# Two attention layers on one core: a new order of the side work in the first seven steps, and a last batch whose halves lie in separate PSUM banks

## The chip, the core and the metric

The kernel runs on one core of one Trainium2 chip. The core has five engines that each work through a queue of their own in order: TensorE (PE in the profile, its weight loads PEld), VectorE (DVE), ScalarE (ACT), GpSimd (POOL) and SyncE (SP, which here only starts DMAs). They wait for one another through semaphores. Matmul results land in PSUM, eight banks of 128 partitions x 512 fp32 values, from where DVE and ACT copy them to SBUF. The metric is the device time of one execution in microseconds (us).

## What is computed

Two cross-attention layers follow each other for 8 batches of 256 tokens with 320 channels, in fp32, with 20 heads of 16 channels. The context has 256 rows of 512 channels. Layer 0 attends to 77 text rows and 179 image rows with two separate softmaxes and adds the two results. Layer 1 attends to 252 text rows; its 4 image rows get scores to which a semantic term is added, and a mask per token.

```python
# layer 0
q, k, v       = heads(x @ Wq.T), heads(text @ Wk.T), heads(text @ Wv.T)
k_ip, v_ip    = heads(ip @ Wk_ip.T), heads(ip @ Wv_ip.T)
x1 = (attend(q, k, v) + attend(q, k_ip, v_ip)) @ Wo.T + bo + x
# layer 1
probs_t  = softmax(q1 @ k_t.T * scale)
text_out = probs_t @ v_t
qsem     = l2norm(probs_t @ text_ehs)
fused    = q1 @ k_ip.T * scale + 0.5 * (qsem @ l2norm(ip_ehs).T)
probs_ip = softmax(fused) * spatial_mask[:, None]
out = (text_out + probs_ip @ v_ip) @ W_out + b_out + x1
```

The norm of qsem is not computed from qsem itself: the kernel multiplies the probabilities with the Gram matrix of the text rows (l1_gram) and sums the product with the probabilities.

## The kernel before

The 20 heads of a batch are cut into five quads of four heads. The main loop runs over n = 0 to 45. Step n < 40 does quad n % 5 of batch n // 5 in layer 0, and layer 1 follows six steps behind (SHIFT), so that steps 6 to 39 do a quad of each layer (both_layers) and steps 40 to 45 only layer 1 (layer_1). After the loop, l1_end finishes the last batch.

A layer-0 step goes as follows. The scores of four heads are computed on TensorE into four PSUM banks sc0 to sc3 (line 359), from queries that POOL has masked (qz, line 349). DVE takes maxima (500), ACT exponentials (512), TensorE transposes the probabilities in the same banks (397), DVE copies three heads and ACT the fourth to SBUF (404, "et"), and l0_values multiplies them with v (530, "oT"), which ACT copies to SBUF (540). The next step transposes that result back (550, "o"). Layer 1 has the same frame; its products y (752, 755) take value and Gram columns together from the tile gv, and DVE reads y (759, 763).

Everything that is not a step of a quad is a filler: projections (l0_q, l0_k, l0_v, l1_q, l1_k, l1_v), Gram matrices (l1_gram), the projections of the image rows for all batches at once (ip_squares, ip_norm, ip_T, ip_k, ip_v), and the ends of batches (l0_attn_T, l0_out, l1_probs, l1_probs_T, l1_text, l1_attn, l1_out). The function fillers(n, place) holds a table of places by step, written by hand; steps 0 to 7 have tables of their own. In both_layers place 0 comes after the scores, maxima and half of the exponentials of the step, place 1 after the first two transposed heads and l0_attn, place 2 after the last two. Directly after place 2 the kernel issues the masked queries on POOL, those of layer 1 for this step and those of layer 0 for the next one:

```python
        fillers(n, 2)
        part(l1_values, v1, 2)
        qz[1] = queries(1, n)
        qz[0] = queries(0, n + 1)
```

l1_gram(b, c) works on one half of the 252 text rows: four matmuls (621), ACT multiplies of the result into gv (630; three for c = 0, one for c = 1), and a POOL copy that repeats these columns for the other nine pairs of heads (634; 3402 columns for c = 0, 1134 for c = 1). ip_norm takes a square root on ACT, which loads another activation table (250). The order of PE, DVE, ACT and POOL is as written in the code; the framework sets the waits. Small PSUM results share two banks (mm_tile).

l1_end adds text and image results in PSUM. Its steps text, image, keep and project handle both halves (two times 128 tokens): text transposes attention rows into a bank, image adds the image rows' part, keep copies the sums to SBUF, half 0 on DVE and half 1 on ACT, and project multiplies with the output weights. Heads 0 to 15 (chunks 0 and 1) are done first, heads 16 to 19 (chunk 2) last. Both halves' sums lie in one bank, and so do both halves of pT, the transposed image probabilities.

Of the kernel before, what the change touches and what calls it, by code (L numbers as in the profile page):

```python
# [8 lines left out]
F32 = mybir.dt.float32  # L9
AF = mybir.ActivationFunctionType  # L10
ALU = mybir.AluOpType
# [39 lines left out]
def kernel(  # L51
# [40 lines left out]
    def mm_tile(name):  # L92
        return ps_mm.tile([P, 512], F32, tag="mm", name=name)
# [515 lines left out]
    def l1_gram(b, c):  # L609
        r = bat[b]  # L610
        encT_b = r["encT"]
        if c == 0:
            r["gv"] = [
                bp.tile([TC1, NPAIR, w + 2 * WV], F32, tag=f"gv{i}", name=f"gv{i}_{b}")
                for i, w in enumerate((3 * TC1, TC1))
            ]
        gv = r["gv"][c]
        ps = mm_tile(f"g{c}_{b}")
        n = TXT1 - c * TC1
        for k in range(NE):  # L620
            nc.tensor.matmul(  # L621
                ps[:TC1, :n],
                encT_b[:, k, c * TC1 : (c + 1) * TC1],
                encT_b[:, k, c * TC1 : TXT1],
                start=(k == 0),
                stop=(k == NE - 1),
            )
        blocks = ((TC1, 2.0), (0, 1.0), (TC1, 2.0)) if c == 0 else ((0, 1.0),)
        for i, (t0, f) in enumerate(blocks):
            nc.scalar.mul(  # L630
                gv[:, 0, WV + i * TC1 : WV + (i + 1) * TC1], ps[:TC1, t0 : t0 + TC1], f
            )
        n = len(blocks) * TC1
        nc.gpsimd.tensor_copy(
            gv[:, 1:, WV : WV + n],
            bc(gv[:, 0, WV : WV + n].unsqueeze(1), [TC1, NPAIR - 1, n]),
        )
# [98 lines left out]
    def l1_transposed(u, j, copy=None):  # L736
        transposed_probs(u, j, TC1, u["t0"][j // 2], copy)
# [35 lines left out]
    def by_n(t):  # L773
        n = t.shape[2]
        return bc(t.unsqueeze(3), [P, NH, n, NIP])
# [40 lines left out]
    def l1_probs(b, hs=ALL, eng=nc.gpsimd):  # L816
        r = bat[b]
        fus, g = r["fus"][:, :, hs, :], by_head(r, "gip", b)
        nc.vector.tensor_reduce(g[:, :, hs], fus, AX.X, ALU.add)
        nc.vector.reciprocal(g[:, :, hs], g[:, :, hs])  # L820
        for half in range(NH):
            eng.tensor_scalar_mul(g[:, half, hs], g[:, half, hs], msk[:, half : half + 1])
        eng.tensor_tensor(fus, fus, by_n(g[:, :, hs]), ALU.mult)
# [14 lines left out]
                ALU.mult,  # L838
            )

    def l1_probs_T(b, hs=ALL, ps=None, shared=False):
        r = bat[b]

        rows = hs.stop * NIP
        if ps is None:
            ps = mm_tile(f"pT_{b}")
        for half in range(NH):
            nc.tensor.transpose(
                ps[:rows, half * P : (half + 1) * P],
                r["fus"][:, half, : hs.stop, :].rearrange("p h k -> p (h k)"),  # L850
                ident,
            )
        if "pT" not in r:
            r["pT"] = small.tile([H * NIP, NH * P], F32, tag="pT", name=f"pT_sb_{b}", bufs=1)
        if shared:
            for copy, cols in ((nc.vector.tensor_copy, slice(0, P)), (nc.scalar.copy, slice(P, 2 * P))):
                copy(r["pT"][:rows, cols], ps[:rows, cols])
        else:
            nc.vector.tensor_copy(r["pT"][:rows], ps[:rows, : NH * P])

    def l1_attn(b):
        r = bat[b]
# [24 lines left out]
    def l1_end(b, u):  # L887

        r = bat[b]
        first, last = slice(0, 16), slice(16, H)

        def tile(j, name):
            return ps_sc.tile([P, NH * S], F32, tag=f"sc{j}", name=f"end_{name}")

        def values(j, half):
            l1_values(u, j, (half,))

        def chunk(t, m):
            return t[:, CH[m] : CH[m] + P]

        def text(ps, piece, i, start):
            m, half = piece
            nc.tensor.matmul(
                ps[:, i * P : (i + 1) * P], chunk(r["attn1"][half], m), ident,
                start=start, stop=False,
            )

        def image(ps, ms, hs):
            rows = hs.stop * NIP
            vip = r["vip"].rearrange("p h d -> p (h d)")[:rows]
            for i, m in enumerate(ms):
                nc.tensor.matmul(
                    ps[:, i * S : (i + 1) * S], chunk(vip, m), r["pT"][:rows],
                    start=False, stop=m == ms[-1],
                )

        def keep(ps, ms):  # L920
            n = len(ms)
            v = ps[:, : n * S].rearrange("p (m n s) -> p m n s", m=n, n=NH)
            for half, copy in enumerate((nc.vector.tensor_copy, nc.scalar.copy)):
                copy(aT[half][:, ms[0] : ms[0] + n, :], v[:, :, half, :])

        def project(half, m):
            nc.tensor.matmul(
                o[half][:, :C], aT[half][:, m, :], wo1[:, m, :], start=(m == 0), stop=(m == 2)
            )

        aT = [
            work.tile([P, NC, P], F32, tag="aT", name=f"end_aT_{half}", bufs=2)
            for half in range(NH)
        ]
        o = [tile(2 + half, f"o_{half}") for half in range(NH)]
        sums, sums2 = tile(0, "aT"), mm_tile("end_aT2")
        texts = [(m, half) for m in (0, 1) for half in range(NH)]
        l1_norm(b, first)
        values(0, 0)
        l1_fused(b, first)  # L940
        values(0, 1)
        l1_text(b, first)
        values(1, 0)
        l1_fused_exp(b, first)
        table(AF.Sqrt)
        values(1, 1)
        values(2, 0)
        l1_probs(b, first)
        for i in range(len(texts)):
            text(sums, texts[i], i, i == 0)  # L950
            if i < 3:
                values(*((2, 1), (3, 0), (3, 1))[i])
        l1_norm(b, last)
        l1_text(b, last)
        l1_probs_T(b, first, tile(1, "pT"))
        l1_fused(b, last, nc.vector)
        l1_fused_exp(b, last, nc.vector)
        image(sums, (0, 1), first)
        keep(sums, (0, 1))
        l1_probs(b, last, nc.vector)  # L960
        for half in range(NH):
            text(sums2, (2, half), half, half == 0)
        project(0, 0)
        project(0, 1)
        l1_probs_T(b, last, tile(1, "pT2"), True)
        project(1, 0)
        project(1, 1)
        sums = sums2
        image(sums, (2,), last)
        keep(sums, (2,))  # L970
        for half, eng in enumerate((nc.sync, nc.scalar)):
            project(half, 2)
            osb = work.tile([P, C], F32, tag="attn1", name=f"osb_{b}_{half}", bufs=3)
            nc.vector.tensor_tensor(osb, o[half][:, :C], r["x1"][:, half, :], ALU.add)
            eng.dma_start(out=out[b, half * P : (half + 1) * P, :], in_=osb)
# [24 lines left out]
    def fillers(n, place):  # L1000
# [30 lines left out]
        if n <= NQ + 2:  # L1031
# [3 lines left out]
                    1: [(l0_v, 0, 2)],  # L1035
                },
                {
                    0: [(l0_k, 0, 1)],
                    1: [(l0_k, 0, 2)],
                    2: [(l0_q, 0, (2,))],  # L1040
                },
                {
                    0: [(l1_gram, 0, 0), (l0_v, 1, 0)],
                    1: [(l0_k, 1, 0), (ip_squares, 0)],
                    2: [(ip_norm, 0)],
                },
                {
                    0: [(l0_v, 1, 1), (l0_q, 1, (0, 1))],
                    1: [(ip_T, 0), (l0_v, 1, 2)],
                    2: [(ip_v, 0)],  # L1050
                },
                {
                    0: [(l1_ip, 0), (l1_v, 0, 0), (l1_v, 0, 1)],
                    1: [(ip_k, 0), (l1_gram, 0, 1)],
                    2: [(ip_k, 1)],
                },
                {
                    0: [(l0_k, 1, 1), (ip_k, 2), (l0_q, 1, (2,))],
                    1: [(l1_k, 0, 0)],
                    2: [(l0_attn_T, 0, 0), (l0_attn_T, 0, 1), (l0_out, 0, 0), (l0_out, 0, 1)],  # L1060
                    5: [(l1_xT, 0)],
                    6: [(l1_q, 0, (0, 1))],
                },
                {
                    0: [(l1_k, 0, 1)],
                    1: [(l1_q, 0, (2,))],
                    2: [(l0_k, 1, 2)],
                    4: [(l1_ip, 1), (l1_gram, 1, 0)],
                    5: [(l1_gram, 1, 1)],
                },  # L1070
# [24 lines left out]
            plan[3, 4] = [(l1_k, now, 0)]  # L1095
            plan[4, 0] = [(l1_v, now, 0)]
        if b == B:
            plan[0, 4] = [(l1_k, last, 1)]
            plan[1, 4] = []
        for f, at, *args in plan.get((s, place), ()):  # L1100
            if 0 <= at < B:
# [69 lines left out]
    def layer_1(n, u, v1):  # L1171
# [17 lines left out]
        for pair in range(2):  # L1189
            for head in (2 * pair, 2 * pair + 1):  # L1190
                l1_transposed(u1, head, nc.scalar.copy)
            if n == N0 + SHIFT - 1 and pair:
                l1_den(B - 1)
            part(l1_values, v1, 2 + pair)
            fillers(n, 5 + pair)
# [81 lines left out]
```

## Time and profile before

| | |
|---|---|
| median of three runs | 883.96 us (883.8 to 883.97) |
| the profiled execution, own time | 883.8 us |
| its span in the profile | 882.1 us |
| TensorE busy | 865.1 us |
| VectorE busy | 614.0 us |
| ScalarE busy | 546.0 us |
| GpSimd busy | 208.8 us |
| DMA queues, share of 16 engines, all four | 9.3% |

The profile is of one execution. Its own time is 1.7 us longer than its span, which begins with the first record and ends with the last. A row of a timeline gives the start in us from the begin of the span, the duration, the engine, the line, the operation, the tile written and the tiles read, the shape, the count of merged instructions, and in brackets the idle time ahead of it with what ended it. An fp32 matmul appears as two passes (x2), a transpose as one. Ends of matmuls are modelled, so distances from start to start are safer than durations. In the table of windows, the columns are the window, its length, the busy time of PE, PEld, DVE, ACT and POOL with their counts, the granted TensorE clock, the busy share of the DMA engines and GB/s.

### The profile page before, as it was taken

The numbers are of one execution on the slowest core, as the hardware profiler recorded it, in microseconds if no ns is written. First come the engines' busy times: TensorE is split into PE (matmuls) and PEld (weight loads), VectorE is DVE, ScalarE is ACT, GpSimd is POOL, SyncE is SP. The second block draws the span as 40 slices with busy tenths as digits, with TensorE's granted clock in tenths as the row PEclk, the third lists the DMA queues.
The fourth block names the chain that finished last, engine by engine and source line by source line (L and its number), as shares of the span: only waits on it lengthen the run. The fifth ranks groups of instructions, "written<-read, shape, count | busy, mean of one in ns | idle before, by whom it ended". The sixth has DMA issues, their size and how long they took to land.

```text
span 882.1 us, 18743 instructions
## 1 busy us (share of the span) xinstructions
PE 865.1 (98%) x6178; PEld 696.4 (79%) x6178; DVE 614.0 (70%) x2071; ACT 546.0 (62%) x2386; POOL 208.8 (24%) x376
## 2 busy tenths in 40 slices
PE   9999899999999999999999999999999999999997
PEld 6767678788787887888878888888888787777776
DVE  2544477767777777776778678776777778775765
ACT  4765666656755586555765468654675558654844
POOL 2212311223221222122321322212232122312111
PEclk9999999999999999999999999999999999999999
DMA  9600100001000100011001010000100100000000
GB/s 278 173 6 6 52 2 1 2 16 43 15 2 20 34 25 2 10 27 42 16 1 21 16 43 1 3 20 16 43 1 1 22 16 1 1 21 1 1 20 16
DMA packets 24624, 22.96 MB, mean 26 GB/s; under 512 B 5936, under 2 KB 24496, under 8 KB 24528
## 3 DMA queue, kind: packets, MB, share of 16 engines
q1 hardware_dynamic: 23088, 20.27, 8.7%
q10 hardware_dynamic: 1440, 1.49, 0.5%
q8 instruction: 50, 0.82, 0.4%
q14 instruction: 46, 0.38, 0.1%
HBM read 18.31 MB, written 2.62 MB: 24 GB/s over the span
## 4 chain that ended last, share of the span: by engine, by line
PE 85%; ACT 3%; DVE 1%; issue 0%; POOL 0%; ACTq 0%; DVEq 0%
PE y L752 17%; PE sc L397 15%; PE sc L359 9%; PE y L755 9%; PE v L322 9%; PE k L310 7%; PE q L292 6%; PE p_o L335 5%; PE oT L530 4%; PE g L621 2%; ACT e L728 1%; ACT e L512 1%; PE p_aT_ps L328 1%; PE o L550 1%; PE ipo L866 1%; PE x1T_ps L328 1%
## 5 line engine op out<-in xcount | busy, mean ns | idle before, releaser
L512 ACT ACTIVATE e<-sc,nmx 128x77 f32<-128x77 f32 (+1 forms) x640 | 227.2, 411 | 58.1 <-DVE nmx L500 56.4
L728 ACT ACTIVATE e<-sc,nmx 128x252 f32<-128x252 f32 x320 | 147.4, 484 | 119.5 <-DVE aip L708 106.2
L752 PE MATMUL y<-gv,et 126*128 126x272 f32 x640 | 202.1, 397 | 1.2
L759 DVE CUSTOM_DVE_ANT_0 e<-y,e 128x252 f32<-128x252 f32 x320 | 134.0, 419 | 93.2 <-PE y L755 84.9
L397 PE MATMUL sc<-ident,e 128*126 128x128 f32 (+1 forms) x1280 | 183.2, 274 | 6.2 <-ACT e L512 3.7
L404 DVE COPY et<-sc 128x512 f32<-128x512 f32 (+1 forms) x228 | 153.9, 689 | 24.7 <-PE sc L397 15.5
L500 DVE TENSOR_REDUCE nmx<-sc 128x2 f32<-128x154 f32 x320 | 109.7, 415 | 85.4 <-PE sc L359 85.4
L397 PEld LDWEIGHTS sc<-ident,e 128*126 128x126 f32 (+1 forms) x1280 | 148.7, 140 | 17.6 <-ACT e L512 8.2
L512 ACT ACTIVATION_READ_ACCUMULATOR e<-sc,nmx 128x1 f32 x640 | 159.5, 250 | 0.0
L755 PEld LDWEIGHTS y<-gv,et 126*128 126x128 f32 x640 | 120.7, 189 | 25.9
L755 PE MATMUL y<-gv,et 126*128 126x146 f32 x640 | 131.4, 287 | 0.0
L713 DVE TENSOR_REDUCE nmx<-sc 128x2 f32<-128x504 f32 x160 | 106.7, 674 | 24.2 <-PE sc L359 24.2
L565 POOL TENSOR_TENSOR attn<-o_sb 128x64 f32<-128x64 f32 x80 | 24.4, 327 | 405.4 <-DVE o_sb L555 365.5
L752 PEld LDWEIGHTS y<-gv,et 126*128 126x128 f32 x640 | 104.8, 190 | 18.1 <-issue 3.0
L404 ACT COPY et<-sc 126x512 f32<-126x512 f32 (+1 forms) x92 | 52.9, 593 | 74.2 <-PE sc L397 74.1
L359 PE MATMUL sc<-k,sc_qz 32*128 32x256 f32 x1152 | 82.5, 400 | 1.0 <-POOL sc_qz L349 1.0
L349 POOL TENSOR_SCALAR sc_qz<-q,quad_m 128x256 f32<-128x256 f32 x80 | 73.2, 925 | 7.3 <-ACT q L299 6.7
L359 PEld LDWEIGHTS sc<-k,sc_qz 32*128 32x128 f32 x1152 | 52.0, 184 | 24.4 <-issue 14.8
L728 ACT ACTIVATION_READ_ACCUMULATOR e<-sc,nmx 128x1 f32 x320 | 69.8, 218 | 0.0
L322 PE MATMUL v<-wv,encT 128*126 128x324 f32 (+1 forms) x192 | 58.1, 447 | 0.0
L763 DVE COPY num<-y 128x20 f32<-128x20 f32 x320 | 55.8, 174 | 0.0
L335 PE MATMUL p_o<-wo,p_aT 128*128 128x320 f32 x180 | 53.0, 437 | 0.3 <-DVE p_aT L329 0.3
(151 smaller groups left out, 1047.1 us busy)
## 6 DMA issues: line engine op xcount, KB each, us to landing
encT<-in_encT_dram SPq DMA_DIRECT2D x7, 512.0 KB
x<-in_x_dram SPq DMA_DIRECT2D x8, 320.0 KB
out_dram<-osb SPq DMA_DIRECT2D x15, 160.0 KB
xT<-in_xT_dram SPq DMA_DIRECT2D x7, 256.0 KB
texts<-in_encT_dram SPq DMA_DIRECT2D x6, 154.0 KB
xT<-in_xT_dram SPq DMA_DIRECT2D x7, 128.0 KB
vip_rows<-vipA SPq DMA_DIRECT2D x32, 25.0 KB
wv<-in_WvT_dram SPq DMA_DIRECT2D x1, 640.0 KB
```

What stands on the lines that cost most here:

```text
L322: nc.tensor.matmul(ps, lhsT(k), w[:, k, :], start=(k == 0), stop=(k == NE - 1))
L335: nc.tensor.matmul(ps[:, :C], aT[:, m, :], w[:, m, :], start=(m == 0), stop=(m == NC - 1))
L359: nc.tensor.matmul(sc[j][:, half, :], qz[rows, half * P : (half + 1) * P], kT(j)[rows, :], start=True, stop=True,)
L397: nc.tensor.transpose(v[:, c, half, :], u["e"][x][:, i, half, t0 + c * tn : t0 + (c + 1) * tn], ident,)
L404: copy(u["et"][x][:tn, i].rearrange("p c n s -> p (c n s)"), ps)
L500: nc.vector.tensor_reduce(u["nmx"][x][:, j, :, a], u["sc"][2 * x + j][:, :, t0:t1], AX.X, ALU.max, negate=True,)
L512: nc.scalar.activation(u["e"][x][:, j, half, t0:t1], u["sc"][2 * x + j][:, half, t0:t1], AF.Exp, bias=u["nmx"][x][:, j, half, a : a + 1], ...
L713: nc.vector.tensor_reduce(u["nmx"][x][:, j, :], u["sc"][2 * x + j][:, :, t0 : t0 + TXT1], AX.X, ALU.max, negate=True,)
L728: nc.scalar.activation(u["e"][x][:, j, half, t0 : t0 + TXT1], u["sc"][2 * x + j][:, half, t0 : t0 + TXT1], AF.Exp, bias=u["nmx"][x][:, j, ...
L752: nc.tensor.matmul(y, et[:, 1 - odd, half, :], gv[0][:, g, full], start=True, stop=False)
L755: nc.tensor.matmul(y[:, into], et[:, odd, half, :], gv[1][:, g, part], start=False, stop=True)
L759: nc.vector.tensor_tensor_reduce(e, y[:, g0 : g0 + TXT1], e, op0=ALU.mult, op1=ALU.add, scale=1.0, scalar=0.0, accum_out=r["n2"][:, half, ...
```

## The change

It has two parts. The first deals out the fillers of steps 1 to 6 anew. The q projection of columns of chunk 2 goes from place 2 to place 0 of step 1, l1_gram(0, 1) from place 1 of step 4 to place 2 of step 1, l1_gram(0, 0) from place 0 to place 2 of step 2, and further projections come one place or one step earlier or later. l1_gram allocates gv at whichever of its calls comes first.

```diff
                 {
-                    0: [(l0_k, 0, 1)],
+                    0: [(l0_k, 0, 1), (l0_q, 0, (2,))],
                     1: [(l0_k, 0, 2)],
-                    2: [(l0_q, 0, (2,))],
+                    2: [(l1_gram, 0, 1)],
                 },
                 {
-                    0: [(l1_gram, 0, 0), (l0_v, 1, 0)],
+                    0: [(l0_v, 1, 0), (l0_v, 1, 1)],
                     1: [(l0_k, 1, 0), (ip_squares, 0)],
-                    2: [(ip_norm, 0)],
+                    2: [(ip_norm, 0), (l1_gram, 0, 0)],
                 },
                 {
-                    0: [(l0_v, 1, 1), (l0_q, 1, (0, 1))],
-                    1: [(ip_T, 0), (l0_v, 1, 2)],
+                    0: [(l0_q, 1, (0, 1)), (ip_T, 0)],
+                    1: [(l0_v, 1, 2)],
                     2: [(ip_v, 0)],
                 },
                 {
                     0: [(l1_ip, 0), (l1_v, 0, 0), (l1_v, 0, 1)],
-                    1: [(ip_k, 0), (l1_gram, 0, 1)],
-                    2: [(ip_k, 1)],
+                    1: [(ip_k, 0), (ip_k, 1)],
+                    2: [(ip_k, 2)],
                 },
                 {
-                    0: [(l0_k, 1, 1), (ip_k, 2), (l0_q, 1, (2,))],
+                    0: [(l0_k, 1, 1), (l0_q, 1, (2,))],
                     1: [(l1_k, 0, 0)],
...
                 {
-                    0: [(l1_k, 0, 1)],
-                    1: [(l1_q, 0, (2,))],
-                    2: [(l0_k, 1, 2)],
+                    0: [(l1_k, 0, 1), (l1_q, 0, (2,))],
+                    1: [(l0_k, 1, 2)],
```

The second part concerns the steps after layer 0 has ended, and l1_end. In step 40, l1_k of the last batch's second chunk goes from place 4 to place 0, ahead of the o transposes (l0_attn). In step 43, l1_probs_T and l1_text of batch 6 go from place 5, between the two pairs of heads, to a new place 7 behind the transposes of the second pair.

```diff
         if b == B:
-            plan[0, 4] = [(l1_k, last, 1)]
+            plan[0, 0] = [(l1_k, last, 1)]
+            plan[0, 4] = []
+            plan[3, 7], plan[3, 5] = plan[3, 5], []
             plan[1, 4] = []
...
                 l1_transposed(u1, head, nc.scalar.copy)
+            if pair:
+                fillers(n, 7)
```

In l1_end, the sums of the two halves get a bank each (sc0 and sc1 for chunks 0 and 1, the two mm banks for chunk 2), and so do the two halves of the last pT (the two banks of y). Each half's copy follows its own transposes. image issues one matmul of 128 columns per half and chunk instead of one of 256 per chunk. Two texts come ahead of the value product (2, 1) instead of one. image and keep of chunk 2 come ahead of project(1, 1) instead of behind it. Where l1_probs runs on DVE (the last four heads), mask and 1/sum are applied by one fused instruction per half, in place of two multiplies of the sums and one of the probabilities.

```diff
+        if eng is nc.vector:
+            for half in range(NH):
+                f = fus[:, half]
+                eng.scalar_tensor_tensor(
+                    f, f, msk[:, half : half + 1], by_n(g[:, :, hs])[:, half], ALU.mult, ALU.mult
+                )
+            return
...
-        for i in range(len(texts)):
-            text(sums, texts[i], i, i == 0)
-            if i < 3:
-                values(*((2, 1), (3, 0), (3, 1))[i])
+        text(sums, 0, 0)
+        text(sums, 0, 1, 1)
+        values(2, 1)
+        text(sums, 1, 0)
+        values(3, 0)
+        text(sums, 1, 1, 1)
+        values(3, 1)
...
-        l1_probs_T(b, last, tile(1, "pT2"), True)
+        l1_probs_T(
+            b, last,
+            [ps_y.tile([P, W2], F32, tag="y", name=f"end_pT2_{half}") for half in range(NH)],
+            copies,
+        )
         project(1, 0)
+        image(sums2, (2,), last)
+        keep(sums2, (2,))
         project(1, 1)
-        sums = sums2
-        image(sums, (2,), last)
-        keep(sums, (2,))
```

More of the change, by code (lines that the diff above doesn't have):

```diff
@@ L611, in l1_gram @@
         encT_b = r["encT"]
-        if c == 0:
+        if "gv" not in r:
             r["gv"] = [
@@ L839, in l1_text, with l1_probs_T @@
             )
-    def l1_probs_T(b, hs=ALL, ps=None, shared=False):
+    def l1_probs_T(b, hs=ALL, ps=None, copies=None):
         r = bat[b]
         rows = hs.stop * NIP
+        whole = mm_tile(f"pT_{b}") if ps is None else None
         if ps is None:
-            ps = mm_tile(f"pT_{b}")
+            ps = [whole[:, half * P : (half + 1) * P] for half in range(NH)]
+        if "pT" not in r:
+            r["pT"] = small.tile([H * NIP, NH * P], F32, tag="pT", name=f"pT_sb_{b}", bufs=1)
         for half in range(NH):
             nc.tensor.transpose(
-                ps[:rows, half * P : (half + 1) * P],
+                ps[half][:rows, :P],
                 r["fus"][:, half, : hs.stop, :].rearrange("p h k -> p (h k)"),
@@ L852, in l1_probs_T @@
             )
[L853 to L859, printed above, removed]
+            if copies:
+                copies[half](r["pT"][:rows, half * P : (half + 1) * P], ps[half][:rows, :P])
+        if not copies:
+            nc.vector.tensor_copy(r["pT"][:rows], whole[:rows, : NH * P])
     def l1_attn(b):
@@ L902, in chunk, with text @@
             return t[:, CH[m] : CH[m] + P]
-        def text(ps, piece, i, start):
-            m, half = piece
+        copies = (nc.vector.tensor_copy, nc.scalar.copy)
+        def text(ps, half, m, i=0):
             nc.tensor.matmul(
-                ps[:, i * P : (i + 1) * P], chunk(r["attn1"][half], m), ident,
-                start=start, stop=False,
+                ps[half][:, i * P : (i + 1) * P], chunk(r["attn1"][half], m), ident,
+                start=i == 0, stop=False,
             )
@@ L913, in image @@
             vip = r["vip"].rearrange("p h d -> p (h d)")[:rows]
[L914 to L918, printed above, removed]
+            for half in range(NH):
+                for i, m in enumerate(ms):
+                    nc.tensor.matmul(
+                        ps[half][:, i * P : (i + 1) * P], chunk(vip, m),
+                        r["pT"][:rows, half * P : (half + 1) * P],
+                        start=False, stop=m == ms[-1],
+                    )
         def keep(ps, ms):
             n = len(ms)
-            v = ps[:, : n * S].rearrange("p (m n s) -> p m n s", m=n, n=NH)
-            for half, copy in enumerate((nc.vector.tensor_copy, nc.scalar.copy)):
-                copy(aT[half][:, ms[0] : ms[0] + n, :], v[:, :, half, :])
+            for half, copy in enumerate(copies):
+                copy(
+                    aT[half][:, ms[0] : ms[0] + n, :],
+                    ps[half][:, : n * P].rearrange("p (m s) -> p m s", m=n),
+                )
         def project(half, m):
@@ L935, in l1_end @@
         o = [tile(2 + half, f"o_{half}") for half in range(NH)]
-        sums, sums2 = tile(0, "aT"), mm_tile("end_aT2")
-        texts = [(m, half) for m in (0, 1) for half in range(NH)]
+        sums = [tile(half, f"aT_{half}") for half in range(NH)]
         l1_norm(b, first)
@@ L948, in l1_end @@
         l1_probs(b, first)
-        for i in range(len(texts)):
-            text(sums, texts[i], i, i == 0)
-            if i < 3:
-                values(*((2, 1), (3, 0), (3, 1))[i])
+        text(sums, 0, 0)
[5 more added lines that the diff above has]
+        values(3, 1)
         l1_norm(b, last)
         l1_text(b, last)
-        l1_probs_T(b, first, tile(1, "pT"))
+        l1_probs_T(b, first)
         l1_fused(b, last, nc.vector)
@@ L960, in l1_end @@
         l1_probs(b, last, nc.vector)
+        sums2 = [mm_tile(f"end_aT2_{half}") for half in range(NH)]
         for half in range(NH):
-            text(sums2, (2, half), half, half == 0)
+            text(sums2, half, 2)
         project(0, 0)
         project(0, 1)
-        l1_probs_T(b, last, tile(1, "pT2"), True)
+        l1_probs_T(
+            b, last,
+            [ps_y.tile([P, W2], F32, tag="y", name=f"end_pT2_{half}") for half in range(NH)],
+            copies,
+        )
         project(1, 0)
+        image(sums2, (2,), last)
+        keep(sums2, (2,))
         project(1, 1)
-        sums = sums2
-        image(sums, (2,), last)
-        keep(sums, (2,))
         for half, eng in enumerate((nc.sync, nc.scalar)):
```

## The prediction

> **What bounds the kernel now.** I read the busy table first, then the chain that ended last, then busy time by step. TensorE works 98% of the span and is 85% of the chain, so time is lost or won only where TensorE stands still.
>
> ```profile
> PE 865.1 (98%) x6178; PEld 696.4 (79%) x6178; DVE 614.0 (70%) x2071; ACT 546.0 (62%) x2386; POOL 208.8 (24%) x376
> ...
> PE 85%; ACT 3%; DVE 1%; issue 0%; POOL 0%; ACTq 0%; DVEq 0%
> ```
>
> The view by windows, cut where each step's scores start (steps 1 to 6 of the main loop), has as columns: window, length, busy PE, PEld, DVE, ACT, POOL, granted clock, DMA share, GB/s.
>
> ```profile
> 22.50:33.66 11.16, 10.27 (x90) 8.53 (x89) 5.31 (x13) 8.79 (x40) 1.50 (x3) 1.00 0.87 227
> 33.66:44.90 11.24, 11.19 (x83) 8.52 (x83) 7.03 (x15) 8.86 (x40) 5.57 (x7) 1.00 0.44 113
> 44.90:59.70 14.80, 14.29 (x95) 9.84 (x95) 7.56 (x19) 9.62 (x40) 3.29 (x6) 1.00 0.00 1
> 59.70:71.38 11.68, 11.40 (x92) 8.79 (x91) 5.50 (x15) 8.11 (x43) 2.64 (x4) 1.00 0.13 11
> 71.38:91.52 20.14, 18.53 (x129) 14.51 (x125) 8.44 (x20) 8.34 (x39) 5.86 (x14) 1.00 0.06 17
> 91.52:110.33 18.81, 16.35 (x133) 12.40 (x129) 10.06 (x24) 13.83 (x62) 5.94 (x7) 1.00 0.15 49
> ```
>
> Busy TensorE includes modelled ends, so I count idle from start to start in the timeline. Unhindered, a step's scores take 1.07 us, one head's four transposes 0.44, a k projection 2.11 to 2.22, a q column block 1.30, l0_v 2.15 to 2.26, gram 0 1.81, gram 1 0.93, ip_k 0.81, oT 1.00. That leaves idle 1.51, 1.14, 0.92, 0.62, 2.68 and 4.13 us in the six steps, 11.0 in all. Most is transposes that wait for ACT's exponentials. Nothing else can be won there, since the matmuls stay the same and change places only.
>
> **The fillers: what moves on the other queues.** Each gram issues matmuls, ACT multiplies into gv, and one POOL broadcast (L634). Its two calls go to place 2 of steps 1 and 2. The masked queries (qz, L349) of the *next* step are issued on POOL right after place 2, and the next scores wait for them. In the order of the changed kernel, L634 stands directly ahead of qz in both steps. Before, gram 0 stood at place 0:
>
> ```profile
> 39.33 3.02 POOL L634 COPY gv<-gv 126x3402 f32<-126x3402 f32 x1 [8.46 <-ACT gv L630]
> 42.32 1.04 POOL L565 TENSOR_TENSOR attn<-o_sb 128x64 f32<-128x64 f32 x2
> 43.34 0.92 POOL L349 TENSOR_SCALAR sc_qz<-q,quad_m 128x256 f32<-128x256 f32 x1
> ...
> 69.15 1.13 POOL L634 COPY gv<-gv 126x1134 f32<-126x1134 f32 x1 [0.91 <-ACT gv L630]
> ```
>
> The large broadcast takes 3.02 us, the small 1.13, and qz 0.92 more. Before, both ended in time: the scores followed at 44.90, after an oT that ACT's copy set.
>
> *Step 1* (scores at 22.50). The q block moved to place 0 fills TensorE's waits before the second and third transpose group, but its ACT scaling delays the later exponentials by 0.28. Last transposes end at 31.29, gram 1 at 32.2. ACT still owes the k(2) copies (1.52) and the et copy of the fourth head (32.32 to 32.91). As after the same copy elsewhere (end 43.87, scores 44.90), oT ends 1.03 later: 33.94. The gv multiply follows the et copy, 32.82; POOL starts 0.41 after that (68.74 to 69.15), 33.23; qz starts 1.11 later and takes 0.93, 35.27; scores at 35.32. Idle 2.24: 0.86 around oT and head 4, 1.38 for qz.
>
> *Step 2.* Two l0_v (4.30), heads, o (0.22), k (2.11), then gram 0, start 44.81, end 46.62, and oT until 47.62. ACT has the et copy at 45.0, and then, ahead of the gv multiplies, ip_norm's table load:
>
> ```profile
> 43.88 1.28 ACT L250 ACT_TABLE_LOAD   x1
> 45.18 0.20 ACT L250 ACTIVATE ip_rn<-ip_rn 32x1 f32<-32x1 f32 x1
> ```
>
> So the load runs 45.61 to 46.89, the multiplies start at 47.02, and POOL 0.71 later as before (38.62 to 39.33), 47.73; qz from 50.72 to 51.65; scores at 51.70. TensorE stands from 47.62: 4.08 us. Behind qz nothing else on TensorE can run, since place 0 of step 3 comes after its scores.
>
> *Step 3.* Its q and ip_T fill 4.3 us after the scores start. The Exp table is loaded after the first maxima (1.28 in the row of before), so heads 0 and 1 are ready at +4.79 and +6.19: idle 0.53 and 0.96, with 0.11 more 1.60. *Step 4*: ip_k takes gram 1's place; head 3 waits for ACT as before, 0.60. *Step 5*: ip_k and its wait for DVE (0.44) are gone; ACT's copies no longer wait for q (1.00 before), so head 3 is ready at +8.4 instead of about +9.5. Idle 2.36, of which 1.80 is the unchanged chain attn_T, out, x1T. *Step 6*: q moves ahead of the heads. Heads 1 and 3 wait 0.46 and 0.37, the layer-1 scores 1.2 for an et copy now queued behind six k copies, the later heads 0.96: 2.97.
>
> Sum: 2.24 + 4.08 + 1.60 + 0.60 + 2.36 + 2.97 = 13.85 against 11.0: **+2.85**. The two qz stalls cost 5.46, the relief elsewhere gives 2.61.
>
> **A rule that speaks against it.** Here the granted clock stays 1.00 through all steps, whose longest single TensorE gap is 0.96. At the end the last matmul finishes at 878.58 and the clock is half from 880.2:
>
> ```profile
> 880.20:880.40 0.20, 0.00 (x0) 0.00 (x0) 0.00 (x0) 0.00 (x0) 0.00 (x0) 0.50 1.11 397
> ```
>
> At the start, eight 256-column passes took 3.78 us, 0.47 each, against 0.22 later (2.59 for twelve). The Trainium skill, "TensorE: Matmul & The Clock Gate", Part 1, says that an idle window of about 3.4 us halves the clock until a busy window has passed, and that the window runs freely. By the rows alone the 4.08 us gap costs itself. By the rule it can cost half of up to 3.4 us more, 1.7, less what hides in step 3's 1.5 us of waiting. My estimate from that page, between 0 and 1.7, is **+0.8**, about what the scores alone would lose at half speed (1.07).
>
> **Layer 1's last steps.** Two recorded waits go:
>
> ```profile
> 791.37 0.44 PE L550 MATMUL o<-ident,oT_sb 128*128 128x128 f32 x2 [0.55 <-ACT oT_sb L540]
> ...
> 838.05 0.42 PE L848 MATMUL pT<-ident,fus 128*80 128x128 f32 x2 [0.65 <-POOL fus L823]
> ...
> 876.26 0.60 PE L915 MATMUL end_aT<-pT_sb,vip 80*128 80x256 f32 x2
> 877.24 1.34 PE L927 MATMUL end_o<-wo,end_aT 128*128 128x320 f32 x4 [0.38 <-DVE end_aT L924]
> ```
>
> l1_k(7,1), 1.70 us, goes ahead of the o transposes and covers the 0.55. Scores come 1.1 later, but 7 us of queued matmuls lie between them and the first use of their exponentials. Its k copies on ACT and POOL are short and early. Moving probs_T behind two transpose groups (0.87) covers the 0.65: POOL's fus ends at 837.99, the new transposes start at 838.27; pT_sb is copied by about 839.2, and ipo follows at 839.9. l1_text moves too, ahead of a qz needed 13 us later. Without cover each wait would stand: 0 back.
>
> **The end by halves.** Before, DVE and ACT copy one bank in turn (pT 875.38 to 875.66, then 875.70; aT 876.89, then 877.22). The Trainium skill, "PSUM — Partial Sum Buffer", "PSUM bank collisions raise a hardware error", asks that engines be kept apart by bank and quadrant; separate banks would by that remove two turns of 0.32, 0.64 in all. But the row shows TensorE busy with project(1,0) and (1,1) until 876.26, so the first turn was hidden. Anew: pT starts near 875.03, project(1,0) ends at 875.79, image's two matmuls of 0.22 at 876.24, project(1,1) at 876.78, where the last projections start: 0.46 earlier than 877.24. The fused multiply saves some 0.2 on DVE, behind TensorE's projections. Against it, two texts now precede value (2,1), so the last values, and the chain norm, Exp load, exp, come 0.22 later; fus would be ready at 874.70 with TensorE free at 874.95, so hidden by 0.25. The image matmuls are eight passes of 128 columns instead of four of 256: the same 0.9 to 1.05. Bounds: -0.46 to +0.2; I take -0.3. **Layer 1 in all: -0.55 - 0.65 - 0.3 = -1.5.**
>
> **The sum.** +2.85 + 0.8 - 1.5 = +2.15 on the profiled execution's own 883.8 us (span 882.1): **886.0**. The median 883.96 is 0.16 above that execution.
>
> **Rivals.** (1) *The stalls without the clock, and the end's whole gain*: +2.85 - 1.8 = +1.05, **884.9**. For it: the waits are sure, the half clock shows only at the end of this trace. (2) *The reliefs of steps 5 and 6 don't come* (1.09 and 1.16), since other exponentials or the et copy end last there: 886.0 + 2.25 = **888.2**. For it: ACT is busy 13.8 of 18.8 us in step 6; against it, the waits removed are in the rows. (3) *The other side*: POOL's broadcast does not hold the scores. The place is POOL's queue before qz in steps 1 and 2; the price is 5.46 plus the 0.8. Then -2.61 - 1.5 = -4.1, **879.7**. It turns to faster than before once the two stalls with any clock loss sum to under 4.1, for instance if the broadcast took a third of its 3.02 and the gv multiplies ran ahead of the table load. Against it: sixteen broadcasts in the trace keep to 1.13 or 3.02, and the order is plain.
>
> **Chances.** Forecast 0.58, rival 1 0.20, rival 2 0.14, rival 3 0.08. Change is told from none here at about 0.2%, 1.77 us: slower means above 885.7, faster below 882.2. The forecast's own range, with the clock cost 0 to 1.7 and the end's bounds, is 884.9 to 887.3; 0.42 of its 0.58 lies above 885.7. With rival 2 and a little of rival 1: slower 0.58, same 0.35, faster 0.07. The range for 8 in 10 runs from within rival 1 with small savings to rival 2: 883.9 to 888.3.
>
> **What would show it.** In the new trace: scores of step 2 near 35.3 and of step 3 near 51.7, each released by POOL's qz, with L634 just before; a wait "sc <- sc_qz" of some 5 us in TensorE's waits where it was 0.6; a granted clock below 1.00 after 51 us if the rule bites; scores of step 7 about 3 us later than 110.33; no wait at pT or o in the last steps; the last projections 0.5 earlier after the last values. If the scores of step 3 come before 48 us the forecast is wrong.

## The result and the profile after

The changed kernel takes **886.31 us** (median of 10 runs, 885.41 to 886.81), the kernel before 883.9 us on the same chip (10 runs, 883.47 to 884.14). The ratio is 1.0026 with a 95% interval of 1.0018 to 1.0035: slower by 2.4 us, more than the 0.2% from which on a change can be told from none here. The profiled execution took 885.41 us, with a span of 883.7. The medians of the kernel before differ by chip (883.87 to 884.46), so each experiment below stands against the kernel before on its own chip. One execution in experiment 2 (step 1 only) ran at a mean granted clock of 0.556 and took 1468 us; it is left out, and that kernel has no profile at full clock.

The busy table and the chain of waits of the changed kernel:

```profile
PE 865.0 (98%) x6184; PEld 697.0 (79%) x6184; DVE 611.8 (69%) x2070; ACT 545.4 (62%) x2386; POOL 208.7 (24%) x376
...
PE 92%; ACT 4%; issue 2%; DVE 1%; DMA 1%; POOL 1%; SPq 0%; DVEq 0%; ACTq 0%; POOLq 0%
```

TensorE's busy time is the same as before to 0.1 us. No engine has more work, so the loss is waiting (and slower matmuls, as will be seen). The windows, cut again where the scores of steps 1 to 6 start:

```profile
22.72:35.27 12.55, 11.33 (x98) 9.44 (x97) 5.21 (x13) 9.05 (x42) 2.63 (x4) 1.00 0.73 210
35.27:51.72 16.45, 12.43 (x91) 9.61 (x91) 6.58 (x18) 9.82 (x42) 4.97 (x5) 1.00 0.27 71
51.72:65.29 13.57, 13.57 (x86) 9.14 (x87) 6.17 (x16) 8.37 (x36) 3.87 (x8) 0.87 0.01 1
65.29:76.97 11.68, 11.38 (x92) 8.77 (x91) 5.69 (x16) 8.00 (x42) 1.50 (x3) 1.00 0.13 11
76.97:96.00 19.03, 17.48 (x120) 13.52 (x117) 8.24 (x19) 8.23 (x39) 5.86 (x14) 1.00 0.07 19
96.00:113.89 17.89, 16.75 (x132) 13.06 (x129) 10.12 (x24) 13.63 (x62) 5.93 (x7) 1.00 0.16 52
```

Step 2 stands out: 16.45 us long with 12.43 of TensorE work. Step 3 shows the opposite sign of trouble: TensorE is busy for all of it, and the granted clock column has 0.87. A full busy column there is slow work, not much work. Over the six steps the sum is 91.17 us, against 87.83 before: 3.34 lost. POOL's timeline around the two starts:

```profile
33.18 1.13 POOL L634 COPY gv<-gv 126x1134 f32<-126x1134 f32 x1 [2.88 <-ACT gv L630]
34.29 0.92 POOL L349 TENSOR_SCALAR sc_qz<-q,quad_m 128x256 f32<-128x256 f32 x1
...
47.71 3.05 POOL L634 COPY gv<-gv 126x3402 f32<-126x3402 f32 x1 [3.60 <-ACT gv L630]
50.74 0.92 POOL L349 TENSOR_SCALAR sc_qz<-q,quad_m 128x256 f32<-128x256 f32 x1
```

and TensorE's, where the brackets name what it waited for:

```profile
35.27 1.15 PE L359 MATMUL sc<-k,sc_qz 32*128 32x256 f32 x16 [1.22 <-POOL sc_qz L349]
...
46.62 1.07 PE L530 MATMUL oT<-et,v 128*32 128x256 f32 x16
51.72 1.47 PE L359 MATMUL sc<-k,sc_qz 32*128 32x256 f32 x16 [4.03 <-POOL sc_qz L349]
```

Read the two together: the queries need only 0.92 us on POOL, but they stand behind a broadcast that no score reads. In step 2 the broadcast itself waits for ACT (3.60 idle, ended by gv), so TensorE is idle from the end of oT at 47.69 until 51.72. The last row also shows the clock: sixteen score matmuls take 1.47 us instead of 1.15. The window with the low clock:

```profile
52.50:55.60 3.10, 3.10 (x14) 2.04 (x7) 2.42 (x8) 1.55 (x3) 1.44 (x2) 0.50 0.00 0
```

At the other end of the kernel the two waits at o and at pT are gone (no bracket in these rows of TensorE):

```profile
796.09 0.38 PE L550 MATMUL o<-ident,oT_sb 128*128 128x128 f32 x2
...
841.07 0.38 PE L859 MATMUL pT<-ident,fus 128*80 128x128 f32 x2
...
874.48 1.16 PE L926 MATMUL end_aT<-pT_sb,vip 64*128 64x128 f32 x8 [0.83 <-DVE pT_sb L867]
...
877.41 0.70 PE L941 MATMUL end_o<-wo,end_aT 128*128 128x320 f32 x2
877.95 0.61 PE L926 MATMUL end_aT<-pT_sb,vip 80*128 80x128 f32 x4
878.40 1.78 PE L941 MATMUL end_o<-wo,end_aT 128*128 128x320 f32 x6
```

The two copies of the last pT now follow each half's own transposes, 0.11 apart, where before the second began when the first had ended (0.32 apart):

```profile
877.50 0.29 DVE L865 COPY pT_sb<-end_pT 80x128 f32<-80x128 f32 x1 [0.66 <-PE end_pT L859]
```
```profile
877.61 0.26 ACT L865 COPY pT_sb<-end_pT 80x128 f32<-80x128 f32 x1 [1.38 <-PE end_pT L859]
```

The same two copies in the kernel before:

```profile
875.38 0.28 DVE L857 COPY pT_sb<-end_pT 80x128 f32<-80x128 f32 x1 [0.67 <-PE end_pT L848]
```
```profile
875.70 0.26 ACT L857 COPY pT_sb<-end_pT 80x128 f32<-80x128 f32 x1 [1.57 <-DVE pT_sb L857]
```

### The profile page after: what moved, and what is told of

It is laid out like the page before. It is cut to its first block, busy times and chain, and to the rows that moved or that the text cites. A ratio compares the mean times of both kernels' runs of the same rounds, so it can differ in the third digit from the quotient of the medians.

```text
span 883.7 us, 18756 instructions
## 1 busy us (share of the span) xinstructions
PE 865.0 (98%) x6184; PEld 697.0 (79%) x6184; DVE 611.8 (69%) x2070; ACT 545.4 (62%) x2386; POOL 208.7 (24%) x376
## 4 chain that ended last, share of the span: by engine, by line
PE 92%; ACT 4%; issue 2%; DVE 1%; DMA 1%; POOL 1%; SPq 0%; DVEq 0%; ACTq 0%; POOLq 0%
PE y L752 17%; PE sc L397 15%; PE v L322 11%; PE sc L359 10%; PE y L755 9%; PE k L310 7%; PE q L292 7%; PE p_o L335 6%; PE oT L530 4%; ACT e L512 2%; PE g L621 2%; PE p_aT_ps L328 1%; ACT e L728 1%; PE o L550 1%; PE ipo L874 1%
```

## The experiments

The theory: the first part of the change loses by two stalls at qz behind the broadcast, and by the clock that falls in the longer one; the second part wins 1.5 to 2 us. The rivals: the stalls hide a loss that would come anyway, since other fillers are badly placed; the low clock costs nothing beside the gap; the second part wins nothing.

**1. Both broadcasts behind the queries.** l1_gram is split; the broadcast becomes l1_repeat, which runs at place 3, after the queries have been issued. All else is the changed kernel.

```diff
                 {
...
                     1: [(l0_k, 0, 2)],
-                    2: [(l1_gram, 0, 1)],
+                    2: [(l1_gram, 0, 1, True)],
+                    3: [(l1_repeat, 0, 1)],
                 },
...
-                    2: [(ip_norm, 0), (l1_gram, 0, 0)],
+                    2: [(ip_norm, 0), (l1_gram, 0, 0, True)],
+                    3: [(l1_repeat, 0, 0)],
```

> The changed kernel with the two POOL broadcasts of gv issued just after the masked queries instead of just before them; nothing else moves. Theory (the broadcasts hold up the queries in POOL's queue): the two waits of TensorE for qz, 1.2 and 4.0 us, go, the granted clock stays at 1.00, and the time falls from 886.3 to 880.6 (880.0 to 881.2), under the kernel before. Rival (ACT ends last in these steps whatever POOL does: its table load, the et copy): the scores come at most 1 us earlier, and the time stays above 885.

Measured: 880.5 us (880.28 to 880.65) against 884.46, ratio 0.9954 (0.9942 to 0.9967). It beats both kernels. POOL's timeline and TensorE's of this kernel:

```profile
43.04 0.92 POOL L349 TENSOR_SCALAR sc_qz<-q,quad_m 128x256 f32<-128x256 f32 x1
46.67 3.05 POOL L639 COPY gv<-gv 126x3402 f32<-126x3402 f32 x1 [2.71 <-ACT gv L630]
```
```profile
34.21 1.15 PE L359 MATMUL sc<-k,sc_qz 32*128 32x256 f32 x16
...
45.58 1.07 PE L530 MATMUL oT<-et,v 128*32 128x256 f32 x16
46.58 1.15 PE L359 MATMUL sc<-k,sc_qz 32*128 32x256 f32 x16
```

The broadcast takes as long as ever and starts after the scores it used to hold. The scores follow oT without a bracket, at 46.58 instead of 51.72, and the mean granted clock of all five executions is 1.00. Steps 1 to 6 last 85.62 us here (scores from 22.93 to 108.55), 2.21 less than before. So the other new places win; the order on one queue is what loses.

**2. Each broadcast alone.** The same edit in step 2 only, then in step 1 only.

> The changed kernel with the large broadcast alone (step 2) behind the masked queries. Theory: the 4.0 us wait and the half clock go, the 1.2 us wait of step 1 stays: 4.7 us under the changed kernel (4.2 to 5.2), some 2.5 under the kernel before, narrow spread. Rival (the two waits are one delay that only moves on): less than 3 us under the changed kernel.

> The changed kernel with the small broadcast alone (step 1) behind the masked queries. Theory: 1.2 us under the changed kernel, the 4.0 us gap, the half clock and a spread of over 1 us stay. Rival (step 2's gap takes the 1.2 us up, since ACT's chain ends there at its own time): no more than 0.4 us under the changed kernel.

On one chip, with the changed kernel run beside them: changed kernel 885.86, step 2 only 880.95 (880.85 to 881.3), step 1 only 884.79 (884.13 to 885.39), before 883.87. The large broadcast costs 4.9 us, the small one 1.1; together 6.0. The first is more than its 4.03 of waiting, the second about its 1.22. Without the large broadcast alone the changed kernel is already 2.9 us faster than the kernel before. In the kernel with the large broadcast late, step 3 is:

```profile
47.58:60.85 13.27, 12.20 (x90) 8.20 (x86) 6.69 (x18) 8.77 (x38) 6.98 (x9) 1.00 0.00 1
```

Full clock, 1.07 of waiting, and 13.27 us long: this is step 3 without the penalty.

**3. The gap kept, the clock held up.** Seven unused matmuls fill the gap of step 2; their results are read by nothing. The wait for qz stays.

```diff
         if n == 2:
+            ps = mm_tile("warm")
+            for i in range(7):
+                nc.tensor.matmul(ps[:, :S], ident, wq[:, 0, 0:S], start=True, stop=True)
             twice(wkip1, wq1)
```

> The changed kernel with seven unused matmuls of 256 columns (3.0 us) on TensorE inside the 4.0 us gap of step 2. They are not part of the computation and change no output. Theory (the gap halves the clock for a window that runs freely, and the loss varies with its phase): granted clock 1.00 in step 3, median down from 886.3 to 885.4, and the runs within 0.7 us of each other as before instead of 1.4. Rival (the clock costs nothing, the spread comes from elsewhere): 886.3 and a spread of 1.4.

Measured: 885.81 us (885.53 to 886.03, 21 runs) against 884.46, ratio 1.0014 (1.0008 to 1.0021). TensorE's timeline and the window of step 3:

```profile
47.09 1.07 PE L530 MATMUL oT<-et,v 128*32 128x256 f32 x16
48.09 3.29 PE L1243 MATMUL warm<-wq,ident 128*128 128x256 f32 x14
52.19 1.15 PE L359 MATMUL sc<-k,sc_qz 32*128 32x256 f32 x16 [0.81 <-POOL sc_qz L349]
```
```profile
52.19:65.49 13.30, 12.21 (x86) 8.20 (x86) 6.27 (x16) 8.40 (x36) 3.86 (x8) 1.00 0.01 1
```

The scores still come 4.03 us after oT has ended (48.16 to 52.19), but step 3 is 13.30 long at full clock, like 13.27 above. The loss against the kernel before is 1.35 us, where the changed kernel loses 2.0 to 2.4 on two chips: 0.6 to 1.1 us on the medians is the fallen clock. The intervals of these ratios overlap at their edges, so the windows of step 3 carry the reading more than the medians do. Experiment 8 parts the executions by their clock.

**4. The changed kernel again,** on another chip.

> The changed kernel once more, beside the next two on one chip. Theory: 2.4 us (1.7 to 3.1) over the kernel before, its runs spread over more than 1 us. If it lies 1.4 over and within 0.7 us, the unused matmuls of the earlier run have saved nothing and the clock costs nothing.

Measured: 885.86 us (885.19 to 887.29) against 883.87, ratio 1.0025 (1.0015 to 1.0034). The ratio repeats, but the runs lie 2.1 us apart, where experiment 3's lay 0.5 apart. The profiled execution took 887.21. Its TensorE timeline, and then its windows:

```profile
52.16 2.09 PE L359 MATMUL sc<-k,sc_qz 32*128 32x256 f32 x16 [4.03 <-POOL sc_qz L349]
```
```profile
52.16:67.12 14.96, 14.96 (x86) 10.27 (x86) 6.18 (x16) 8.54 (x36) 3.87 (x8) 0.79 0.00 1
55.40:58.40 3.00, 3.00 (x9) 2.37 (x8) 1.61 (x5) 2.99 (x13) 0.00 (x0) 0.50 0.00 0
```

The gap is the same 4.03, yet all the scores run at half speed (2.09 instead of 1.15), the clock is still half at 58.40, and step 3 lasts 14.96: 1.69 over the 13.27 at full clock. In the first profile it lasted 13.57, or 0.30 over. One gap, two prices; what sets which is the subject of experiment 8.

**5. Gram before the table load.** In step 2, l1_gram runs before ip_norm, so that ACT multiplies into gv ahead of the table load. This is one of the two conditions that the prediction's third rival named.

```diff
-                    2: [(ip_norm, 0), (l1_gram, 0, 0)],
+                    2: [(l1_gram, 0, 0), (ip_norm, 0)],
```

> The changed kernel with l1_gram(0, 0) ahead of ip_norm in place 2 of step 2, so that ACT multiplies into gv before it loads the square root's table. Theory (the table load ends last by about 0.25 us, gram's matmuls just before it): the broadcast starts 0.2 to 0.4 us earlier against the scores of its own step, and the gap shrinks from 4.0 to 3.7. Rival (the 1.28 us of the load are all on the path): the gap shrinks by over 1 us.

Measured in one execution: 886.11 us. TensorE's timeline, and ACT's:

```profile
51.43 2.09 PE L359 MATMUL sc<-k,sc_qz 32*128 32x256 f32 x16 [3.85 <-POOL sc_qz L349]
```
```profile
46.62 0.61 ACT L630 ACTIVATE gv<-g 126x126 f32<-126x126 f32 x3 [1.06 <-PE g L621]
```

The broadcast starts 2.58 us after the gram matmuls instead of 2.88, but the gap shrinks by 0.18 only, as the qz row of this execution takes 1.09 instead of 0.92. ACT now stands idle for 1.06 us until the gram matmuls have ended, so the table load had hidden most of that wait and was a small part of the stall. Whether the time is better can't be told from one execution of a kernel that varies by 2 us.

**6. The two parts of the change apart.** First layer 1's steps and the end by halves alone, with the old tables for steps 1 to 6; then the new tables alone, with the old end.

> The kernel before with the change's second part alone (steps 40 and 43, and the end by halves). Theory (the two parts add): 1.7 us under the kernel before, 882.2. Rival (the gain of the end comes only because the later steps were shifted by the front): within 0.5 us of 883.9.

> The kernel before with the change's first part alone (fillers of steps 1 to 6). Theory: the front costs 3.3 us without the half clock and up to 1 more with it, 888.0 (887.3 to 888.6). Rival (the front costs nothing by itself): under 885.

Measured against 884.46: the end alone 882.7 (882.28 to 883.29), ratio 0.9979 (0.997 to 0.9988), or -1.76 us. The front alone 888.97 (888.34 to 889.7), ratio 1.005 (1.0038 to 1.0063), or +4.5. In us the front alone lies above the 887.3 to 888.6 that was expected, but this chip's kernel before is 0.6 above the 883.9 meant there; as a difference it is inside. The sum of both, +2.75, lies 0.3 to 0.8 above the whole change's +2.0 to +2.4. That is within these intervals. The profiled execution of the front alone:

```profile
52.23:67.22 14.99, 14.99 (x86) 10.25 (x87) 6.18 (x16) 8.59 (x36) 3.86 (x8) 0.79 0.00 1
```

It paid the high price of experiment 4, and so did three of the other four by their clock (table in experiment 8).

**7. The end part cut in two.** One kernel has only the two moved blocks:

```diff
         if b == B:
-            plan[0, 4] = [(l1_k, last, 1)]
+            plan[0, 0] = [(l1_k, last, 1)]
+            plan[0, 4] = []
+            plan[3, 7], plan[3, 5] = plan[3, 5], []
...
+            if pair:
+                fillers(n, 7)
```

> The kernel before with the two moved blocks alone (l1_k in step 40, probs_T and text in step 43). Theory: the two waits of 0.55 and 0.65 go and nothing else waits: 1.2 to 1.4 us under the kernel before. Rival (one wait comes back at the next use of the same bank or of k1): at most 0.7 under.

The other has only the separate banks, the fused multiply and the new order in l1_end.

> The kernel before with l1_end by halves alone. Theory: the last projections start 0.4 us earlier after the last value products: 0.3 to 0.5 us under the kernel before. Rival (both waits of ACT for DVE were on the path): 0.65 or more under. Other side (two texts ahead of value (2, 1) delay the last values by 0.22, uncovered): not under it.

Measured against 884.04: blocks 882.61 (882.29 to 883.01), ratio 0.9982 (0.9974 to 0.999), or -1.43, at the edge of the expected 1.2 to 1.4; halves 883.39 (883.23 to 883.83), ratio 0.9992 (0.9984 to 1.0), or -0.65, with an interval that reaches no change. That interval holds both the expected 0.3 to 0.5 and the rival's 0.65 or more, so the median can't tell them apart. TensorE's timelines of the blocks alone and of the halves alone:

```profile
792.78 0.38 PE L550 MATMUL o<-ident,oT_sb 128*128 128x128 f32 x2
...
837.76 0.38 PE L848 MATMUL pT<-ident,fus 128*80 128x128 f32 x2
```
```profile
872.44 1.16 PE L926 MATMUL end_aT<-pT_sb,vip 64*128 64x128 f32 x8 [0.83 <-DVE pT_sb L867]
...
875.37 0.70 PE L941 MATMUL end_o<-wo,end_aT 128*128 128x320 f32 x2
875.91 0.61 PE L926 MATMUL end_aT<-pT_sb,vip 80*128 80x128 f32 x4
876.36 1.78 PE L941 MATMUL end_o<-wo,end_aT 128*128 128x320 f32 x6
```

Both waits are gone without the rest of the change. In the halves kernel the time from value (2, 0) to project(0, 2) is 9.47 us, as in the changed kernel, against 9.89 before: -0.42. By the trace it is the expectation that holds, not the rival.

**8. How long the clock stays low.** In windows of 0.1 us the moment of the fall and of the return can be read off. By then four profiles had the gap, and the long stretch had come whenever the scores began after the fall. Two more executions of the changed kernel tested that.

> The changed kernel once more, for the clock after the gap of step 2. In the four profiles with this gap, half clock lasted 3.4 us where the scores of step 3 had started before the clock fell, and 6.8 us where they started after it had fallen (by 0.4 to 1.2 us). Theory: the clock comes back after a stretch of about 3.4 us, counted from the fall, in which TensorE never stands; a stretch with 0.4 us of standing in it does not count. Then here too: fall after the start of the scores gives 3.3 to 3.5 us and a step 3 of 13.4 to 14.0 us; fall before it gives 6.7 to 6.9 us and a step 3 of 14.5 to 15.0 us. Rival: the length has nothing to do with the order of the two; then the pairs mix.

> The same kernel and the same reading as after_third, with another phase if chance gives one: half clock of 3.3 to 3.5 us if the scores of step 3 start before the clock falls, 6.7 to 6.9 us if they start after.

Measured: 886.54 and 886.46 us. The windows of the first, at the fall, at the return, and over step 3:

```profile
50.70:50.80 0.10, 0.00 (x0) 0.00 (x0) 0.00 (x0) 0.00 (x0) 0.10 (x2) 0.74 0.00 0
57.50:57.60 0.10, 0.10 (x2) 0.10 (x1) 0.00 (x0) 0.10 (x2) 0.00 (x0) 0.62 0.00 0
51.71:66.42 14.71, 14.71 (x87) 10.11 (x87) 6.18 (x16) 8.48 (x36) 3.86 (x8) 0.80 0.00 1
```

A mean of 0.74 falling to 0.50 puts the fall at 50.75; 0.62 rising to 1.00 puts the return at 57.58. All six profiles with the gap, read in this way:

| profile | clock falls | scores start | clock returns | half for | step 3 | over 13.27 |
|---|---|---|---|---|---|---|
| changed kernel, first | 52.41 | 51.72 | 55.82 | 3.41 | 13.57 | 0.30 |
| changed kernel, experiment 4 | 51.71 | 52.16 | 58.54 | 6.83 | 14.96 | 1.69 |
| front alone | 51.85 | 52.23 | 58.68 | 6.83 | 14.99 | 1.72 |
| gram first | 50.26 | 51.43 | 57.09 | 6.83 | 14.60 | 1.33 |
| changed kernel, third profile | 50.75 | 51.71 | 57.58 | 6.83 | 14.71 | 1.44 |
| changed kernel, fourth profile | 50.66 | 51.63 | 57.49 | 6.83 | 14.70 | 1.43 |

Both came out as the theory said, though both are of the long kind. In these six profiles half clock lasts 3.41 us where TensorE is already at work when the clock falls, and twice that where it still stands, by 0.4 us or by 1.2. So a stretch of 3.41 us that begins with some standing did not bring the clock back; the next one did.

Only one short case was read row by row, so that its order of fall and start is the cause remains a reading. That there are two lengths does not rest on it: the record has the mean granted clock of every execution, and half clock for 3.41 us of 884 makes a mean of 0.998, for 6.83 us 0.996. The executions with the gap fall into these two groups (two at 0.997 are put with the first):

| kernel | clock 0.997 or 0.998 | clock 0.995 or 0.996 |
|---|---|---|
| changed kernel, result | 3 runs, median 885.50 (885.41 to 885.94) | 7 runs, median 886.47 (885.92 to 886.81) |
| changed kernel, experiment 4 | 4 runs, median 885.43 (885.19 to 885.58) | 5 runs, median 886.48 (885.86 to 887.29) |
| step 1 only, experiment 2 | 7 runs, median 884.32 (884.13 to 884.58) | 13 runs, median 885.23 (884.72 to 885.39) |
| front alone | 1 run, 888.34 | 4 runs, median 889.14 (888.77 to 889.7) |

The groups lie 0.8 to 1.05 us apart. Over the kernel before, the changed kernel loses 1.6 in the first group and 2.6 in the second, on both chips; with the clock held up it lost 1.35 (experiment 3, at a mean clock of 0.999 or 1.00 in all its executions). So the fallen clock costs about 0.2 us or about 1.2.

## Why the prediction was right

The likeliest case came true, in sign, size and mechanism: 886.0 was said, 886.31 measured, and 885.41 for the profiled execution. Step by step:

- **The stalls at qz.** Said: scores of step 2 near 35.3 and of step 3 near 51.7, each behind L634 and qz. They came at 35.27 and 51.72, with stalls of 1.22 and 4.03, where 1.38 and 4.08 were said. Experiment 2 prices them at 1.1 and 4.9 (the second with its clock). Rival 3, that the broadcast doesn't hold the scores, falls by these rows; experiment 1 shows what it would have brought, 880.5 where the rival said 879.7.
- **The front without the clock.** Said +2.85. The six steps lost 3.34, of which 0.30 is clock (13.57 against 13.27 in step 3), so 3.04. The term that was mis-sized is step 6: its relief was taken at 1.16 and is 0.92 (18.81 to 17.89). Step 5 is 1.11 shorter (20.14 to 19.03), but 0.81 of that is an ip_k that went to step 4; its relief in waiting is 0.30. The prediction's own sum has 0.32 for it (2.68 to 2.36), while rival 2 was priced with 1.09: by the sum rival 2 should have read 887.5, not 888.2. Both reliefs came, so it falls either way. Scores of step 7 came at 113.89, 3.56 after 110.33; 0.22 of it had been lost before step 1 began, where this change moves nothing (in the kernels with the old front these scores start between 22.50 and 22.78).
- **The clock.** Said +0.8, between 0 and 1.7. The six profiles show 0.3 to 1.7, five of them 1.3 or more; by the groups of experiment 8 it is about 0.2 or 1.2, and the medians show a mix, 0.6 to 1.1. The first profile has the low price, and its 885.41 us is the lowest of its ten runs. The prediction weighed the row (no price) against the Trainium skill, "TensorE: Matmul & The Clock Gate", Part 1: an idle window of about 3.4 us halves the clock until a busy window has passed, with windows that run freely. The stretches of 3.41 us and the varying price agree. What the estimate missed, as the six profiles read, is that a window which starts with a short stand doesn't count as busy, so that two can pass: the price is not spread evenly from 0 to 1.7. Rival 1 left the clock out and gave 884.9, +1.05; experiment 3, where the clock stays up, loses 1.35, but in the changed kernel the clock did fall.
- **Layer 1's last steps.** Said -0.55 and -0.65, together -1.20. Blocks alone measured -1.43. In the trace of the changed kernel, compared with the shift just before each place, they bring 0.57 and 0.85: the pT term is 0.20 larger than the recorded wait of 0.65. The wait itself was larger than its bracket, which counts from the modelled end of the product ahead of it. TensorE's rows at this place, of the kernel before (its next start is pT, 838.05), and of the changed kernel:

```profile
836.99 0.41 PE L755 MATMUL y<-gv,et 126*128 126x146 f32 x2
```
```profile
839.95 0.41 PE L755 MATMUL y<-gv,et 126*128 126x146 f32 x2
840.19 1.04 PE L397 MATMUL sc<-ident,e 128*126 128x128 f32 x8
```

From start to start it is 1.06 before and 0.24 after, so 0.82 of the 0.85 lies here.
- **The end by halves.** Said -0.3, after -0.46 was worked out and part of it deducted; the trace has -0.42, the medians -0.65. The working had the parts otherwise. From the first image matmul to project(0, 2) the gain is 0.64 (4.46 us instead of 5.10): 0.53 after the last pT, from image and keep ahead of project(1, 1) together with copies not taken in turn, and 0.11 ahead of it. Against it, 0.22 is lost. The prediction had the cause, two texts ahead of value (2, 1) that make the last values 0.22 later, but took it as hidden in front of the last pT. It comes out at the first one: both texts are spent, so nothing on TensorE covers DVE's copy, and image waits 0.83 (shown with the profile after) instead of the 0.61 of the kernel before:

```profile
872.14 1.13 PE L915 MATMUL end_aT<-pT_sb,vip 64*128 64x256 f32 x4 [0.61 <-DVE pT_sb L859]
```

The fused multiply, the banks and the new order were not tried apart, so which of them brings the 0.64 stays open.

What was luck: the 0.8 for the clock lies between two prices and no execution seems to have paid it; the median is near 886.0 because seven of ten paid the high one. The profiled execution paid 0.3 and came out 0.6 below the forecast. Step 1 (12.55 us long instead of 12.82) and the gains in layer 1 (1.76 by the end alone, instead of 1.5) erred in the direction opposite to step 6 and to the 0.22 lost ahead of step 1, so the sum is nearer than its terms.

## What to carry to other kernels

Before a block moves, write out what it issues on every engine, and look at what comes next in each of those queues: here two copies that nobody needed for tens of microseconds cost their length or more (1.1 us for one of 1.13, 4.9 for one of 3.05 that also waited for ACT), because they stood ahead of the next step's operand. When the work itself is well placed, split it and move only the late part, as experiment 1 did. The gap of 4 us on TensorE cost more than its length, and filling it with unused matmuls saved 0.2 to 1.2 us, closing it 4.9. And a step whose busy share rises to 100% at a granted clock of 0.87 or 0.79 has not got more work.

## What was not expected of the hardware

That the price of one gap of about 4 us takes two separate values: 0.3 us of slow clock in the profile where it falls after work has begun again, 1.3 to 1.7 in the five where it falls before, though the gap is the same to 0.2 us. With it the runs of the changed kernel spread over 2.1 us on one chip, while those of the kernel with the gap filled by unused matmuls (3.29 us of them) spread over 0.5; about 1 us of the difference is the distance of the two groups. By these profiles which comes depends on where the fall lies against the gap, between 2.7 and 4.7 us after TensorE stopped, and no edit here controls that.
